# A sum of two lines of g made ahead of pair 2, and an earlier weight set in pair 7, in a four-layer kernel on one core

## The chip, the cores and the metric

The program runs on one core of a Trainium2 chip. The metric is device time in microseconds for one execution. A core has TensorE (PE in the profile), VectorE (DVE), ScalarE (ACT), GpSimd (POOL) and SyncE (SP). Each takes its instructions in the order in which the program gives them, and they wait for one another through semaphores. Transfers are issued by SP and by POOL (a few by ScalarE), each on a queue of its own, and all of them are carried by the same 16 DMA engines. All numbers in this kernel are float32.

## What is computed

x is [1024, 16, 16, 16]. Four layers follow one another, each of them x = x + f(groupnorm(x)) with 8 groups of 2 channels:

```
_gn(v):  g = v.reshape(B, 16, 16, 8, 2); (g - mean) / sqrt(var + 1e-5), over h, w and the 2 channels
layer 0: f = a linear map of the 4096 values of a sample, given as three cores
         core0 [1,16,16,16], core1 [16,16,16,16], core2 [16,16,16,1] (rank, out, in, rank)
layers 1 and 3: per pixel, two 3x3 depthwise filters, 48 -> 128 -> 16 dense with a relu, and a mask
layer 2: a 3x3 convolution over the 16 channels, with a bias
```

The change touches layer 0 and the preparation of layer 3's weights, which happens during layer 0.

## The kernel before

**Layer 0 as products of blocks.** The 4096x4096 matrix of layer 0 is never stored whole. The kernel splits input and output into blocks and needs 26 products of sums of blocks, taken two at a time: 13 *pairs*, numbered from 0, in the table `OUTER`. A pair has four *units* (q = 0 to 3), numbered through, so that unit u = 4 j + q belongs to pair j. A unit makes seven inner products (`INNER`, k = 0 to 6), each in two halves: 14 steps of a unit, numbered 0 to 13, and 56 of a pair (`pieces`, with the matmuls of L1567). One pair takes about 102.5 us.

**The weights of a unit.** What multiplies x is built on the way. From core1 and core2 the kernel makes once, during pair 0, a tensor g that has four *lines* (0 to 3), and stores it in DRAM, in two arrangements: `g_dram[0]` holds lines 0 and 2 side by side, and 1 and 3; `g_dram[1]` holds 0 and 1, and 2 and 3. For a unit, `gload` (L1438, L1440) fetches those lines that the pair's entry in `OUTER` names: a tile of 256 KB holds two lines in its 128 rows. `build` (L1459) multiplies each tile with small coefficients R, made from core0 by `coefs`, and sums over the tiles in PSUM; four copies on ScalarE (L1464) bring the result to SBUF as w. A pair with one or two lines needs one tile in each build, and one with three or four lines needs two: the second goes to a fixed place in the second of the two big tiles of x. There are two builds a unit (h = 0 and 1), for the unit that comes next.

**Sums around the products.** VectorE makes sums of w, s2, s5, s1, s7 and w01 (`mix`, L1489 and L1491), adds the products up from PSUM to r (`gather`, L1603, L1613; some of it is copied by ScalarE, L1609, L1611), and makes a pair's extra inputs from its four blocks of x (`combined`, L1203): E0, E1 and E2, which the fourth to sixth inner products of each unit read, and two blocks changed in place. `combined` of a pair is placed inside its first unit, two operations after each of steps 1, 3, 5, 7 and 9. The result r is stored to the residual xf in DRAM by `store`: from SP the first time (L1543), by an adding transfer from POOL later (L1541). Where a sign or a sum is needed, a `neg` tile is made first (L1527, L1534).

**Work woven in.** `run` gives out the steps of a pair and puts other lists of steps in between, each with a stretch of the pair (`lo` to `hi`, as shares of it); a plain number in such a list is idle time to be kept. So the order of the instructions on each engine is fixed when the program is built. In pair 1 that other work is the second half of the input: 8 loads of 1 MB from POOL's queue (L1074), their statistics on VectorE (BN_STATS, L1086), transposes on TensorE (L1092), copies of them by ScalarE into a `lines` tile (L1102), and stores of these from SP (L1104); and, at its end, `part_steps(2)`, the inputs of pair 2. Tiles with the tag t4 have four buffers of 512 KB in all of layer 0; `lines`, `neg` and `piece` tiles share them. Transposes and builds share PSUM banks: one bank m, and four banks w, all four of which a build takes.

**The weight sets.** `set1` and `set3` are the two lists of steps that prepare the weights of layers 1 and 3 (`nca_weights`); set3 works in the room behind the blocks of x of the even pairs, where E0 to E2 of pair 8 come to stand, and is woven into pair 7 from 0.02 to 0.85 of it. Its last steps are small tensor copies on POOL (`order`, L369), eight stores of zeros to wy (L378), three copies within the room (`copies`, L325), and the stores of pk and kp (`store`, L328 to L330), all on POOL's queue. r of the even units has a fixed place in the same big tile, so that ScalarE's first copy of a unit waits until r of the unit before last has been stored.

## Time and profile before

| | |
|---|---|
| three runs, median | 2743.33 us (2742.66 to 2747.08) |
| the profiled execution | 2746.07 us, of which its span 2744.3 us |
| TensorE, busy | 2675.8 us, 98% of the span |
| VectorE, busy | 1994.9 us, 73% |
| ScalarE, busy | 1241.4 us, 45% |
| pair 1, 185.7 to 288.2 us of the span | TensorE busy for 100.86 of 102.50 us, VectorE for 78.34 |
| pair 2, 288.2 to 391.0 us | TensorE 102.80 of 102.80, VectorE 69.65 |
| DMA | 502.17 MB, 183 GB/s on average |

How to read the profile: a row of a timeline has the start in us from the span's start, how long it took, engine, line, operation, output and inputs, shapes and how many like it stand in a row; in brackets is how long the engine was idle before it, and what released it. Rows of one kind that follow one another closely are merged. Each float32 matmul of the source stands as two matmuls in the trace. A busy share is an average over the whole span, and tells little of any single stage.

### The profile page before, as it was taken

The numbers are of one execution on the slowest core, as the hardware profiler recorded it, in microseconds if no ns is written. First come the engines' busy times: TensorE is split into PE (matmuls) and PEld (weight loads), VectorE is DVE, ScalarE is ACT, GpSimd is POOL, SyncE is SP. The second block draws the span as 40 slices with busy tenths as digits, with TensorE's granted clock in tenths as the row PEclk, the third lists the DMA queues.
The fourth block names the chain that finished last, engine by engine and source line by source line (L and its number), as shares of the span: only waits on it lengthen the run. The fifth ranks groups of instructions, "written<-read, shape, count | busy, mean of one in ns | idle before, by whom it ended". The sixth has DMA issues, their size and how long they took to land.

```text
span 2744.3 us, 47734 instructions
## 1 busy us (share of the span) xinstructions
PE 2675.8 (98%) x19246; PEld 1756.9 (64%) x19246; DVE 1994.9 (73%) x2416; ACT 1241.4 (45%) x2091; POOL 541.3 (20%) x690
## 2 busy tenths in 40 slices
PE   6999999999999999999999999999999999999997
PEld 5888888888888878888778733333333333334344
DVE  8597667867787766667887777658778858756654
ACT  3324222222232222333332276776767756676664
POOL 2000351312122742311331111111113221110000
PEclk8999999999999999999999999999999999999998
DMA  7686788997897687889689764555575866444665
GB/s 254 215 317 227 242 169 214 236 221 188 193 242 193 154 187 180 226 229 263 171 188 257 148 165 102 108 159 122 106 195 83 202 150 143 101 89 116 180 175 209
DMA packets 264796, 502.17 MB, mean 183 GB/s; under 512 B 32804, under 2 KB 100440, under 8 KB 255360
## 3 DMA queue, kind: packets, MB, share of 16 engines
q1 hardware_dynamic: 180752, 338.78, 37.1%
q0 software_dynamic: 83632, 160.22, 33.9%
q8 instruction: 152, 2.49, 0.4%
q14 instruction: 68, 0.56, 0.1%
q10 hardware_dynamic: 192, 0.13, 0.0%
HBM read 280.66 MB, written 223.35 MB: 184 GB/s over the span
## 4 chain that ended last, share of the span: by engine, by line
PE 81%; DVE 8%; DMA 5%; issue 3%; POOL 1%; ACT 1%; SPq 0%; DVEq 0%; POOLq 0%; ACTq 0%
PE po L1567 37%; PE ph L1974 21%; PE po L1803 8%; PE po L1658 5%; PE pw L1459 4%; DMA xn<-in_x_dram 1%; PE po L1667 1%; DVE xn L1174 1%; DMA xf<-r 1%; DMA xn<-xf 1%; DVE xn L1203 1%; PE ptx L1867 1%; DMA L_conv_kp<-xn 1%; DMA xb<-xn 0%; DMA xn<-xn 0%
## 5 line engine op out<-in xcount | busy, mean ns | idle before, releaser
L1977 ACT ACTIVATE hid<-ph,pack 128x512 f32<-128x512 f32 (+1 forms) x1040 | 641.3, 684 | 313.5 <-PE ph L1974 254.3
L1567 PE MATMUL po<-xn,s 128*128 128x256 f32 x3328 | 756.7, 384 | 13.6 <-DVE s L1489 7.2
L1567 PEld LDWEIGHTS po<-xn,s 128*128 128x128 f32 x3328 | 628.5, 191 | 117.5 <-issue 16.7
L1567 PE MATMUL po<-xn,w 128*128 128x256 f32 x2496 | 565.0, 381 | 1.4 <-DVE xn L1203 1.4
L1974 PE MATMUL ph<-xn,wq 32*128 32x512 f32 (+1 forms) x3752 | 518.3, 590 | 1.9 <-DVE u L1815 1.5
L1567 PEld LDWEIGHTS po<-xn,w 128*128 128x128 f32 x2496 | 468.2, 190 | 74.1 <-issue 5.9
L1464 ACT COPY w<-pw 128x512 f32<-128x512 f32 x416 | 213.6, 600 | 454.6 <-PE pw L1459 371.8
L1974 PEld LDWEIGHTS ph<-xn,wq 32*128 32x128 f32 x3752 | 233.6, 184 | 228.9 <-issue 210.0
L1974 PE MATMUL ph<-xn,pack 32*128 32x512 f32 x1288 | 274.2, 607 | 5.6 <-DVE u L1815 1.6
L1489 DVE TENSOR_TENSOR s<-w 128x1024 f32<-128x1024 f32 x208 | 251.2, 1217 | 28.1 <-PE po L1567 24.8
L1803 PE MATMUL po<-hid,pack 128*32 128x512 f32 (+1 forms) x2080 | 256.0, 592 | 0.8 <-ACT hid L1977 0.5
L1815 DVE SCALAR_TENSOR_TENSOR u<-po,pack,xn 128x512 f32<-128x512 f32 (+1 forms) x130 | 96.3, 741 | 168.2 <-PE po L1803 167.1
L1857 POOL DMA_DIRECT2D xf<-u x96 | 82.6, 860 | 618.7 <-DVE u L1855 592.1
L754 DVE TENSOR_TENSOR xn<-xn,m 128x1024 f32<-128x1024 f32 x128 | 150.2, 1217 | 34.7 <-ACT m L777 34.6
L1974 PEld LDWEIGHTS ph<-xn,pack 32*128 32x128 f32 x1288 | 115.6, 184 | 90.7 <-issue 63.1
L1803 PEld LDWEIGHTS po<-hid,pack 128*32 128x32 f32 x2080 | 53.9, 109 | 174.9 <-ACT hid L1977 86.3
L1658 PE MATMUL po<-xn,convw 128*128 128x512 f32 x368 | 163.6, 598 | 0.0
L1203 DVE TENSOR_TENSOR xn<-xn 128x1024 f32<-128x1024 f32 x130 | 152.7, 1215 | 8.0 <-DMA L_conv_kp<-xn 8.0
L1459 PE MATMUL pw<-R,gq 32*128 32x128 f32 x3328 | 143.7, 286 | 7.5 <-DVE small L1116 6.9
L1603 DVE TENSOR_TENSOR r<-r,po 128x1024 f32<-128x1024 f32 x78 | 95.0, 1218 | 72.9 <-PE po L1567 61.0
L1459 PEld LDWEIGHTS pw<-R,gq 32*128 32x128 f32 x3328 | 116.2, 188 | 41.9 <-issue 38.6
L1541 POOL DMA_DIRECT2D xf<-xn x69 | 89.8, 1776 | 251.2 <-DVE xn L1534 71.7
(229 smaller groups left out, 2784.9 us busy)
## 6 DMA issues: line engine op xcount, KB each, us to landing
xn<-xf SPq DMA_DIRECT2D x128, 512.0 KB
xn<-xb SPq DMA_DIRECT2D x36, 1024.0 KB
wq<-L_conv_wy SPq DMA_DIRECT2D x192, 192.0 KB
xf<-xn POOLq DMA_DIRECT2D x69, 512.0 KB, 10.8
piece<-xb SPq DMA_DIRECT2D x64, 512.0 KB
xf<-r POOLq DMA_DIRECT2D x48, 512.0 KB, 12.7
xf<-u POOLq DMA_DIRECT2D x96, 256.0 KB, 4.2
gq<-g_dram SPq DMA_DIRECT2D x94, 256.0 KB
```

The costliest lines, as they stand in the source:

```text
L754: V.tensor_tensor(part, part, m().unsqueeze(1).broadcast_to([P, 2, NB]), op)
L1203: V.tensor_tensor(out, y, z, f)
L1459: T.matmul(pw[r][:, v, i], g[rows, P * (2 * v + i) : P * (2 * v + i) + P], R[rows, k], start=k == 0, stop=k == len(gs) - 1,)
L1464: A.copy(w.rearrange("p b s t m -> p (b s t) m")[:, :, 32 * r : 32 * r + 32].rearrange("p k (v o) -> p v k o", v=2), pw[r].rearrange("p v ...
L1489: V.tensor_tensor(t.rearrange("p s t m -> p (s t m)"), x, y, f)
L1567: T.matmul(po[:, i], matrix(u, what)[:, i, t], x, start=t == 0, stop=t == 3)
L1603: V.tensor_tensor(part, part, po.unsqueeze(2).broadcast_to([P, 2, 2, 256]), ALU.add)
L1658: T.matmul(st["po", h][wh], conv["fw"][:, y], X[:, 16 * wh + h + y - 1], start=y == max(0, 1 - h), stop=y == min(2, S - h),)
L1803: T.matmul(po[32 * j : 32 * j + 32], nca["w1"][:, v], hid[j], start=v == 0, stop=v == 1)
L1815: V.scalar_tensor_tensor(u, po, nca["b1"], X[:, 8 * q + w2, cols(hf)], ALU.add, ALU.add)
L1974: T.matmul(ph, w, x, start=k == 0, stop=k == len(tiles) - 1)
L1977: A.activation(h, ph, AF.Relu, bias=nca["bt"][:, r : r + 1])
```

## The change

Pair 2's entry names lines 0, 1 and 3, and every use of lines 0 and 1 in it has the same coefficient. The changed kernel makes the sum of lines 0 and 1 once and calls it line 4, so that the entry names lines 4 and 3 and a build of pair 2 takes one tile. The sums are made in pair 1, one for each q: two tiles (lines 0 and 2; lines 1 and 3) are fetched from `g_dram[0]` by four transfers of 256 KB on SP into two t4 buffers; one VectorE operation multiplies the first with a constant of each row, `low` (1 in the rows of line 0, and 0 in those of line 2), and adds the second, so that line 0 + line 1 and line 3 stand side by side; two transfers on SP store that to `g_sum`. The four sums are woven into pair 1 from 0.04 to 0.5 of it, with eight us of idle time between each fetch and its sum. `low` is made by one small reduction on VectorE in pair 0. The second part puts the end of set3's stretch in pair 7 from 0.85 to 0.75. Everything else stays as it is, but for the order of woven-in steps that follows from this.

```diff
+    low = cst("low", [P, 1])
...
+    g_sum = dram.tile([4, 2, 4, 2, S, 4 * P], F32, tag="g_sum", name="g_sum")
...
-        ((0, 1, 3), None, ("..++ ..++ .... ....", "+30", "+00 -20"),
+        ((4, 3), None, ("..++ ..++ .... ....", "+30", "+00 -20"),
...
-    UNIT = [(1, 0, 0, 0), (0, 1, 0, 0), (0, 0, 1, 0), (0, 0, 0, 1)]
+    UNIT = [(1, 0, 0, 0), (0, 1, 0, 0), (0, 0, 1, 0), (0, 0, 0, 1), (1, 1, 0, 0)]
...
+        def sum_steps():
+            ts = {}
+            def fetch(q):
+                ts[q] = [
+                    work([P, 2, NB], "t4", name).rearrange("p h b -> p (h b)").rearrange(
+                        "p (o f) -> p o f", o=4
+                    )
+                    for name in ("vs", "vg")
+                ]
+                for h, x in enumerate(ts[q]):
+                    for w in range(2):
+                        nc.sync.dma_start(
+                            x[64 * w : 64 * w + 64],
+                            g_dram[0][h, q, w].rearrange("o s k (t f) -> (s k t) o f", t=2),
+                        )
+            def add(q):
+                t, g = ts[q]
+                V.scalar_tensor_tensor(t, t, low, g, ALU.mult, ALU.add)
+                for w in range(2):
+                    nc.sync.dma_start(
+                        g_sum[q, w].rearrange("o s k (t f) -> (s k t) o f", t=2),
+                        t[64 * w : 64 * w + 64],
+                    )
+            return [
+                x for q in range(4)
+                for x in ((0, lambda q=q: fetch(q)), 8, (1.3, lambda q=q: add(q)))
+            ]
...
-                if pair[1] - pair[0] == 2:
+                if pair == (4, 3):
+                    queue.dma_start(g, g_sum[q, h].rearrange("o s k f -> (o s k) f"))
+                elif pair[1] - pair[0] == 2:
...
+        V.tensor_reduce(low, ident.rearrange("p (w v r) -> p v w r", w=2, v=2)[:, 0], AX.XY, ALU.add)
...
-            (part_steps(2), 0.78, 1.0),
+            (sum_steps(), 0.04, 0.5), (part_steps(2), 0.78, 1.0),
...
-            7: (set3, 0.85),
+            7: (set3, 0.75),
```

In the changed program's own order, the first fetch stands on SP right behind the xf writes of unit 3 (three of 512 KB), and the first sum on VectorE between the w01 mix of unit 4 and the two operations that make E2.

More of the change, by code (lines that the diff above doesn't have):

```diff
@@ L699, in train_setup @@
         ]
-        return sums, cores, early, rest
+        return sums, cores, early, rest, sum_steps
     def line_sum(parts, name, own, dear=False):
@@ L2041, in conv_preact_kernel @@
         stage(es, dict(t4=4, s=2, n=2, w1=1, w0=2, s2=1, s5=1, r=1, gq=2, R=2, A=1), dict(w=4, m=1, o=3))
-        sums, cores, early, rest = train_setup(flats[0][:, 8192:9216])
+        sums, cores, early, rest, sum_steps = train_setup(flats[0][:, 8192:9216])
         tag = ["w"]
```

## The prediction

> **What bounds the kernel now.** I read the page first, then layer 0 alone: the timeline of TensorE (PE), and that of VectorE (DVE) where pair 1 begins. The page says that TensorE is never idle for long:

> ```profile
> PE 2675.8 (98%) x19246; PEld 1756.9 (64%) x19246; DVE 1994.9 (73%) x2416; ACT 1241.4 (45%) x2091; POOL 541.3 (20%) x690
> ...
> PE 81%; DVE 8%; DMA 5%; issue 3%; POOL 1%; ACT 1%; SPq 0%; DVEq 0%; POOLq 0%; ACTq 0%
> ```

> So matmuls taken out of layer 0 count in full, if nothing else comes last there; and whatever makes TensorE wait counts in full too. Timeline of TensorE:

> ```profile
> 64.74 1.17 PE L1459 MATMUL pw<-R,gq 32*128 32x128 f32 x32
> 65.84 1.99 PE L1567 MATMUL po<-xn,s 128*128 128x256 f32 x8
> ...
> 185.75 8.83 PE L1567 MATMUL po<-xn,s 128*128 128x256 f32 x32 [2.80 <-DVE s L1489]
> ...
> 209.47 1.89 PE L1567 MATMUL po<-xn,w 128*128 128x256 f32 x8
> ...
> 214.24 3.62 PE L1567 MATMUL po<-xn,w 128*128 128x256 f32 x16
> ...
> 230.78 1.17 PE L1459 MATMUL pw<-R,gq 32*128 32x128 f32 x32
> ...
> 296.73 0.40 PE L1459 MATMUL pw<-R,xn 32*128 32x128 f32 x8
> 297.06 7.17 PE L1567 MATMUL po<-xn,s 128*128 128x256 f32 x32
> ```

> A build from one tile of g takes 1.10 us from its start to the next matmul (64.74 to 65.84). One of pair 2 starts at 295.06 and ends at 297.06: 2.00 us. Timeline of VectorE early in pair 1, unit 4, which starts at 185.75:

> ```profile
> 202.88 1.22 DVE L1491 TENSOR_TENSOR w<-w 128x1024 f32<-128x1024 f32 x1
> 204.02 2.35 DVE L1203 TENSOR_TENSOR xn<-xn 128x1024 f32<-128x1024 f32 x2
> 206.29 1.22 DVE L1603 TENSOR_TENSOR xn<-xn,po 128x1024 f32<-128x1024 f32 x1
> ```

> It has no idle slot from 165 to 213 us. The pair at 204.02 makes E2, which TensorE wants at 209.47 (step 10). The transfers at that time, queues and their shares, for 196 to 207 us:

> ```profile
> q0 software_dynamic: 493, 3.65, 78.6%
> q1 hardware_dynamic: 492, 0.97, 22.8%
> ```

> All 16 engines are full: POOL's queue carries seven 1 MB loads of x (issued from 181.5 to 187.7, the last landing 21.5 us after its issue), and SP's queue gets 0.97 MB in 11 us.

> [...] 88 KB per us for SP, with 2 KB packets against 8 KB ones, and three xf writes of 512 KB, issued by SP at 192.4, 192.9 and 193.4, have semaphore events that put their landings at 203.6, 209.3 and 210.5. [...] after the 2.80 us of idleness above, 32 matmuls took 8.83 us where 7.17 is usual.

> **The change, part by part.**

> *Builds of pair 2.* Eight builds (4 units by 2 halves) lose one tile of g: 8 x (2.00 - 1.10) = 7.2 us less on TensorE. Pair 2 is bound by it: 102.80 of 102.80 us busy in its window, and VectorE is idle for 33 us of it, so all of this counts. Eight loads of 256 KB go too, and two small VectorE operations of the coefficients; both are hidden, worth 0.

> *The constant `low`.* One TENSOR_REDUCE of 64 values a row: by its nearest row (al_c, 128 values, 0.28 us) about 0.2 us. It stands at 51 us in a stretch where VectorE has no gap and TensorE later waits 1.36 us for it (at 77.38): +0.2.

> *The four sums in pair 1, VectorE's work.* Each is one SCALAR_TENSOR_TENSOR over 128x1024; the nearest row is L1534's, 1.22 us with the next 1.13 behind it. No row has this one's pointer operand and two SBUF inputs; [...] I take 1.14 each, 4.6 in all; from 4 to 6. Alone it would be hidden, as VectorE idles some 24 us in pair 1, all after 213.

> *The first sum's wait.* This is what decides. The sum stands on VectorE right behind the w01 mix (202.88) and ahead of the two E2 operations; its four fetches (1 MB) stand on SP right behind the three xf writes, from about 193.9. In ring order they move after those: the third lands at 210.5, and the fetch at 1.05 MB / 0.39 MB per us (the rate of 209 to 212 us) takes 2.6 more. Call the landing L = 213.1; bounds 211.5 (packets overlapping) and 215. VectorE comes to it at 204.0 and waits 9 us, with E2, a gather, eight BN_STATS and x01 (combined's last) queued behind.
> - E2's first half is done at L + 1.14 + 1.22 = 215.5; TensorE wanted it at 209.47: 6.0 us idle.
> - From E2's start to x01's first half done is 7.2 us (204.02 to 211.26 before): 214.2 + 7.2 = 221.5. TensorE wanted that (step 12) at 214.24: 7.3 us late in all. [...]
> - Mixes and gathers follow in order; s5 of unit 5 is done 17 us after L, when TensorE comes for it: no more.

> *t4 buffers.* Sums and lines share four. By the new program's addresses, the lines tile of the transposes of 226.36 and 228.53 gets the buffer of unit 4's `neg`. That `neg` waits for gathers of the late VectorE: at 231 on ScalarE instead of 220.98. Its fourth xf write was issued 3.3 us later and landed 5.2 after that, so 239.6; then two copies, 240.8. The second copy frees a bank that the next build needs, wanted at 230.78 + 7.4 = 238.2: 2.5 us more. The loss is then 9.9, set by L alone (L - 203.2). Later slots (the other three sums, their stores, the loads of g behind them on SP) come free before they are wanted, by 1 us or more. The last load of x (0.87 us of waiting at 239.65) now shares the engines with 1.5 MB of sums: +0.7. Pair 1: +10.6.

> *set3 sooner.* Ahead of it, pair 8 begins with stalls of 0.79, 2.53, 0.36 and 0.64 us on TensorE (4.3). Their causes, VectorE, ScalarE and POOL:

> ```profile
> 998.30 1.23 DVE L1203 TENSOR_TENSOR xn<-xn 128x1024 f32<-128x1024 f32 x1 [8.01 <-DMA L_conv_kp<-xn]
> ...
> 993.92 0.59 ACT L1609 COPY xn<-po 128x512 f32<-128x512 f32 x1 [16.10 <-DMA xf<-xn]
> ...
> 969.17 2.48 POOL L1541 DMA_DIRECT2D xf<-xn  x2 [2.10 <-ACT w L1464]
> 972.45 1.19 POOL L1541 DMA_DIRECT2D xf<-xn  x1 [0.81 <-DMA L_conv_wy<-xn]
> 980.11 0.61 POOL L328 DMA_DIRECT2D L_conv_pk<-xn  x1 [6.46 <-DMA xn<-xn]
> ```

> The step that stores pk and kp now stands ahead of those three xf writes on POOL, behind one xf<-xr more. It must still wait for copies whose queue of small wy writes is the limit (60 to 70 GB/s at a full DMA share, 960 to 970 us). POOL reaches wy 6.6 us sooner, but the xf<-r writes in front end 3 us later, so the copies land some 2 to 3 us sooner; xf<-xr (0.5 MB) takes that up. Then 1.0 MB of stores and 1.5 MB of xf writes are left, as before, in the other order: kp is early, and VectorE's 8.01 us goes; but the last xf write lands where kp did, near 1000.5 instead of 993.8, and ScalarE's copy (16.10) waits for it. TensorE's step 6 of unit 32, ready at 994.3, starts at 1001.7: 7.4 us of idleness in the place of 4.3, +2.9 or so, and a halved window, +1.7. Bounds: -4.3 (all four stalls go) and +8; I take +4.6.

> *Sum:* -7.2 + 0.2 + 10.6 + 4.6 = +8.2 us. The profiled execution took 2746.07 (span 2744.3, 1.8 around it), 2.7 above the median of the three runs, so +8.2 means 2754.3 for one like it and 2751.5, say 2751, for the median.

> **Rivals.**
> - *The saving stands.* The fetch is in time, so sums hide in VectorE's gaps: needs L below about 205.5. Then -7.2, with 0 to -4.3 from pair 7: 2732 to 2737. For it: sums are only 4.6 us of work. Against: three earlier writes of the same ring land at 203.6 to 210.5. It ends faster. Chance 0.12.
> - *Pair 7 pays.* Pair 1 loses as forecast, but POOL's stores and the xf writes both land before 994: 10.8 - 7.2 - (0 to 4.3) = -1 to +4: 2743 to 2747. It needs the copies to land at about 970. For it: POOL is free sooner; against: wy's rate. Chance 0.20.
> - *A milder first wait*, L near 209 [...]: +6 - 7.2 + 4.6, about +3, 2747. Chance 0.08.
> - *More stalls*: a second buffer or bank cascade, further half-clock windows: above +15, 2759 and more. Chance 0.06.

> **How the numbers follow.** The forecast (2749 to 2757) has 0.54. Something under 5.5 us (0.2%) can't be told from no change by this measurement. Faster 0.12; same 0.20 + 0.08 = 0.28; slower 0.54 + 0.06 = 0.60. The range leaves out the first rival and the last one: 2740 to 2759.

> **What would show it.** A wait of 8 to 10 us on VectorE before its first sum, near 204 us; TensorE idle some 6 us before step 10 of unit 4, then at step 12; PEclk below 1 there; a wait of ScalarE for xf writes near 235 and of a build near 238; builds of pair 2 at 1.10 us; at pair 8's start no wait for kp, and a longer one of ScalarE for xf<-xn. I am wrong if the first sum starts by 206, or if TensorE has no stall where pair 8 begins.

## The result, and the profile after

The changed kernel takes 2750.1 us in the median (2748.34 to 2754.25), the kernel before 2743.44 beside it (2739.81 to 2754.0), in 22 runs each: 1.0022 times as long, with an interval of 1.0016 to 1.0029. It is slower by 4 to 8 us, where +8 was forecast. The profiled execution has a span of 2748.7 us, 4.4 more than that of before; the rest of the difference is in the executions that happened to be profiled, since that of before was 2.6 above its median. Executions of one kernel differ by several us (by 14 in the 22 of before), and a trace is one of them: it shows where that execution lost time, and the ratio of many executions what the kernel takes.

TensorE has less work and more idle time. From the page, the busy times and the chain that ended last:

```profile
PE 2670.0 (97%) x18990; PEld 1751.1 (64%) x18990; DVE 1999.5 (73%) x2419; ACT 1241.7 (45%) x2091; POOL 528.0 (19%) x690
...
PE 82%; DVE 8%; DMA 5%; issue 3%; SPq 1%; ACT 1%; POOL 0%; DVEq 0%; ACTq 0%; POOLq 0%
```

Timeline of TensorE after (start, us, engine, line, operation; in brackets the idle time before, and what ended it). In the changed file the lines named here are 34 to 36 higher: L1603 was L1567, L1495 was L1459, L1126 was L1092.

```profile
208.94 0.65 PE L1126 MATMUL ptin<-ident,xn 128*128 128x128 f32 x4
216.66 3.52 PE L1603 MATMUL po<-xn,w 128*128 128x256 f32 x8 [7.06 <-DVE xn L1237]
...
239.59 0.50 PE L1495 MATMUL pw<-R,gq 32*128 32x128 f32 x6
243.35 1.81 PE L1495 MATMUL pw<-R,gq 32*128 32x128 f32 x26 [3.27 <-ACT lines L1136]
...
308.47 1.17 PE L1495 MATMUL pw<-R,gq 32*128 32x128 f32 x32
309.58 2.64 PE L1603 MATMUL po<-xn,s 128*128 128x256 f32 x11
...
898.97 0.50 PE L288 MATMUL L_conv_pt<-ident,xn 128*16 128x128 f32 x3 [1.67 <-DMA xn<-in_L_conv_fc_w_dram]
...
992.22 7.07 PE L1603 MATMUL po<-xn,s 128*128 128x256 f32 x32
999.13 3.62 PE L1603 MATMUL po<-xn,w 128*128 128x256 f32 x16
1002.67 1.17 PE L1495 MATMUL pw<-R,gq 32*128 32x128 f32 x32
1003.78 7.17 PE L1603 MATMUL po<-xn,s 128*128 128x256 f32 x32
```

Five things stand there. Step 10 of unit 4 waits for 7.06 us. A build stops in its middle for 3.27 us. A build of pair 2 takes 1.11 us (308.47 to 309.58). A new wait of 1.67 us stands at set3's first transpose in pair 7. And pair 8 (992.22) begins without any of the four stalls that it had before. The longest of those four, in the timeline of TensorE before:

```profile
999.58 1.99 PE L1567 MATMUL po<-xn,s 128*128 128x256 f32 x8 [2.53 <-DVE xn L1203]
```

What the wait before step 10 comes from is in the timeline of VectorE after, and what stops the build is in that of ScalarE after:

```profile
202.40 1.22 DVE L1527 TENSOR_TENSOR w<-w 128x1024 f32<-128x1024 f32 x1
214.18 1.28 DVE L718 SCALAR_TENSOR_TENSOR vs<-vs,low,vg 128x1024 f32<-128x1024 f32 x1 [10.56 <-DMA vg<-g_dram]
215.38 2.35 DVE L1237 TENSOR_TENSOR xn<-xn 128x1024 f32<-128x1024 f32 x2
```

```profile
232.19 1.06 ACT L1563 ACTIVATE neg<-xn 128x1024 f32<-128x1024 f32 x1 [1.90 <-DVE xn L1639]
...
242.22 1.07 ACT L1136 COPY lines<-ptin 128x512 f32<-128x512 f32 x2 [5.78 <-DMA xf<-neg]
```

VectorE stands for 10.56 us in front of the first sum, with E2 behind it. The late VectorE delays `neg` (232.19, before at 220.98), its xf write lands at 242.07, and only then may ScalarE write `lines` in the same t4 buffer and free a bank for the build. Around or behind each of the two waits TensorE runs at half its clock. The windows view of the changed kernel has, for each stretch, the busy times of PE, PEld, DVE, ACT and POOL with their instructions, then PEclk (the share of the clock that was granted), DMA share and GB/s:

```profile
212.90:219.80 6.90, 3.15 (x8) 2.53 (x9) 5.62 (x8) 0.00 (x0) 0.00 (x0) 0.51 0.61 167
...
243.60:247.10 3.50, 3.50 (x35) 3.28 (x32) 0.93 (x1) 2.06 (x4) 0.38 (x1) 0.51 1.07 340
```

To see where the time went I compare one kind of mark in the two traces, the first of ScalarE's copies (w from pw) of a unit's first build. Unit 4's mark lies 0.31 us earlier than before, unit 8's 12.52 later, unit 13's 7.49, unit 29's 7.80, unit 31's 9.58 and unit 34's 4.44. So pair 1 lost 12.8 us up to this mark, which lies 0.9 behind the first shorter build; up to unit 13 it got 5.0 back, which is about what seven more shorter builds (0.9 each, 6.3) leave behind a new wait of 0.99 at 352.95; pair 7 lost 1.8, most of it set3's transpose; and the start of pair 8 gave 5.1 back. Counted by its 56 steps, pair 1 runs from 185.75 to 313.17 in the trace before and pair 2 to 428.68: both are longer than the 102.5 us given above, and the two windows of the table there end inside them. Two of pair 2's eight shorter builds lie in pair 1 (before, at 295.06 and 304.17).

### The profile page after: what moved, and what is told of

Read it like the earlier page. It is cut to its first block, busy times and chain, and to the rows that moved or that the text cites. A ratio compares the mean times of both kernels' runs of the same rounds, so it can differ in the third digit from the quotient of the medians.

```text
span 2748.7 us, 47252 instructions
## 1 busy us (share of the span) xinstructions
PE 2670.0 (97%) x18990; PEld 1751.1 (64%) x18990; DVE 1999.5 (73%) x2419; ACT 1241.7 (45%) x2091; POOL 528.0 (19%) x690
## 4 chain that ended last, share of the span: by engine, by line
PE 82%; DVE 8%; DMA 5%; issue 3%; SPq 1%; ACT 1%; POOL 0%; DVEq 0%; ACTq 0%; POOLq 0%
PE po L1603 39%; PE ph L2010 21%; PE po L1839 8%; PE po L1694 5%; PE pw L1495 4%; DMA xn<-xf 1%; DMA xn<-in_x_dram 1%; PE po L1703 1%; DMA xn<-xr 1%; DMA m<-means 1%; DVE xn L1208 1%; PE ptx L1903 1%; DVE s L1525 1%; DMA xb<-xn 0%; DVE u L1851 0%
## 5 line engine op out<-in xcount | busy, mean ns | idle before, releaser
L1603 PE MATMUL po<-xn,s 128*128 128x256 f32 x3328 | 754.6, 383 | 11.4 <-DVE s L1525 8.7
L1603 PEld LDWEIGHTS po<-xn,s 128*128 128x128 f32 x3328 | 627.8, 191 | 113.8 <-issue 16.0
L1603 PE MATMUL po<-xn,w 128*128 128x256 f32 x2496 | 566.9, 382 | 8.7 <-DVE xn L1237 8.7
L1603 PEld LDWEIGHTS po<-xn,w 128*128 128x128 f32 x2496 | 469.2, 190 | 82.4 <-DVE xn L1237 9.2
L1495 PE MATMUL pw<-R,gq 32*128 32x128 f32 x3328 | 140.8, 287 | 11.0 <-DVE small L1150 7.1
L1495 PEld LDWEIGHTS pw<-R,gq 32*128 32x128 f32 x3328 | 115.0, 189 | 45.5 <-issue 38.5
```

Of the source, the lines that this page charges most:

```text
L1495: T.matmul(pw[r][:, v, i], g[rows, P * (2 * v + i) : P * (2 * v + i) + P], R[rows, k], start=k == 0, stop=k == len(gs) - 1,)
L1603: T.matmul(po[:, i], matrix(u, what)[:, i, t], x, start=t == 0, stop=t == 3)
```

## Experiments

In the expectations theories have letters.

- For set3: A, putting it sooner is what takes pair 8's stalls away; B, the step of the forecast, by which it costs 4.6 us; C, the stalls went because TensorE comes there later.
- For pair 1: A, the forecast's, VectorE's wait for a fetch that is late by its place in SP's ring (SP's queue, whose transfers stand in the order of their issue); D, the fetch is late because of the loads of x on POOL's queue, wherever it stands; F, the sums' t4 buffers.
- Waits that an edit could bring: E, for xf writes that come later; G, of TensorE for other inputs, beside the sums' transfers; H, for loads of x that are moved back.

Each kernel was timed beside the kernel before on the same chip, in four groups on four chips, with 5 to 14 runs; so compare the ratios, and medians only roughly. The table gives the ratio to the kernel before with its interval, and from the one profiled execution the lateness in us that arises between two marks: in pair 1 (units 4 to 8), in pair 2 (8 to 13), in pair 7 (29 to 31) and where pair 8 begins (31 to 34).

| | median | ratio | interval | pair 1 | pair 2 | pair 7 | pair 8 |
|---|---|---|---|---|---|---|---|
| the change | 2750.1 | 1.0022 | 1.0016 to 1.0029 | +12.8 | -5.0 | +1.8 | -5.1 |
| sums, set3 at 0.85 | 2749.86 | 1.0016 | 1.0006 to 1.0026 | +14.1 | -6.0 | 0.0 | -2.3 |
| set3 at 0.75 alone | 2743.94 | 1.0000 | 0.9992 to 1.0008 | +1.0 | 0.0 | +1.4 | -5.1 |
| fetch ahead of xf writes | 2750.45 | 1.0022 | 1.0011 to 1.0033 | +10.8 | -5.2 | +1.5 | -5.1 |
| first sum later | 2747.64 | 1.0013 | 1.0005 to 1.0021 | +8.9 | -5.5 | +1.6 | -5.1 |
| loads of x behind fetch | 2746.28 | 1.0007 | 0.9999 to 1.0015 | +7.8 | -4.8 | +1.3 | -5.1 |
| a place of its own | 2754.88 | 1.0035 | 1.0023 to 1.0047 | +16.5 | -5.5 | +1.4 | -5.1 |
| sums from 0.26 | 2742.29 | 0.9995 | 0.9987 to 1.0003 | +5.9 | -5.7 | +1.5 | -5.1 |
| from 0.26, own place | 2742.35 | 0.9993 | 0.9985 to 1.0001 | +4.7 | -6.1 | +2.0 | -5.1 |
| spread into pair 2 | 2755.31 | 1.0037 | 1.0023 to 1.0051 | +5.4 | +6.9 | +1.7 | -5.1 |
| the same, set3 at 0.85 | 2753.22 | 1.0037 | 1.0023 to 1.0052 | +4.7 | +6.8 | 0.0 | -5.1 |
| behind the last load | 2746.66 | 1.0006 | 0.9997 to 1.0014 | +7.7 | -5.7 | +1.6 | -5.1 |
| the same, set3 at 0.85 | 2744.93 | 1.0004 | 0.9996 to 1.0013 | +7.4 | -6.2 | 0.0 | -5.1 |

The kernel with set3 alone has no edit in pair 1 and shows +1.0 there (it waits 0.90 us for a load of x at 202.09), so differences of 1 us in that column mean nothing. Nor is a trace the total: the span of the last kernel's profiled execution is 4.7 us shorter than that of before, and its ratio is 1.0004.

### Each part alone

The sums without the earlier set3:

```diff
-            7: (set3, 0.75),
+            7: (set3, 0.85),
```

> The sums as in the changed kernel, set3 back at 0.85. In the trace of the changed kernel, pair 1 costs 13.9 us, the builds of pair 2 give 7.2 back, and pair 8 begins without the 4.3 us of stalls that it had before, at the price of one new stall of 1.67 us at set3's first transpose. Theory A (putting set3 sooner is what took pair 8's stalls away): the stall at 899 us goes, 4 us of stalls stand at pair 8's start again, and the time is 1 to 4 us above the changed kernel: 2751 to 2754. Theory B, the forecast's step (set3 sooner costs 4.6): 4.6 us below the changed kernel, about 2745.5. Theory C (pair 8's stalls went because TensorE comes there some 8 us later, while POOL's chain does not shift): no stalls at pair 8's start here either, and about 1.7 below the changed kernel, 2748.

And the earlier set3 without the sums, in the kernel before:

```diff
-            7: (set3, 0.85),
+            7: (set3, 0.75),
```

> The kernel before with set3 at 0.75 alone, no sums. Theory A (set3 sooner takes pair 8's stalls away): pair 8 begins with at most 1 us of stalls in the place of 4.3, TensorE waits up to 1.7 us at set3's first transpose near 890 us, and the time is 2 to 4 us below the kernel before: 2739.5 to 2741.5. Theory B, the forecast's step: a wait of ScalarE for an xf write in the place of VectorE's for kp, 7.4 us idle at step 6 of unit 32, 4.6 us slower: 2748. Theory C (TensorE's lateness in the changed kernel did it): within 1.5 us of the kernel before.

The sums alone have most or all of the change's loss (1.0016 times, +4.4 us, from 1.6 to 7.1). Their time lies between those that C (2748) and A (2751 to 2754) named, and so does their trace, with 2.0 us of stalls where pair 8 begins; B's 2745.5 is 4.4 below it. Set3 alone measures 1.0000 with an interval of 2.2 us to each side: the forecast's +4.6 (B) is refuted, and so is a gain of more than 2.2. Its trace has what A said, no stall where pair 8 begins and 1.33 us at the first transpose (893.65), but its time is what C named, and not the 2 to 4 us less of A. Of POOL's chain the traces show two things. pk and kp, now in front of the xf writes, land early, and the xf writes too: in the changed kernel pk and kp at 976.7 to 978.2 and the last xf write at 986.7, against 996.3 to 1000.5 and 993.8 before. And six small selects on POOL, which began 8 us later than before, ended 1 us sooner. Timeline of POOL, before and then after:

```profile
896.39 12.66 POOL L279 TENSOR_SCALAR_AFFINE_SELECT xn<-xn 48x256 f32<-48x256 f32 x6
```

```profile
904.20 3.87 POOL L280 TENSOR_SCALAR_AFFINE_SELECT xn<-xn 48x256 f32<-48x256 f32 x6
```

The single records are 3.78, 0.39, 0.39, 4.78, 1.85 and 1.34 us before, and 0.90, then four of 0.39, and 1.26 after. The one of 4.78 runs from 901.06 to 905.84; what VectorE did then is in its timeline before:

```profile
899.84 1.20 DVE L1603 TENSOR_TENSOR xn<-xn,po 128x1024 f32<-128x1024 f32 x1
900.97 1.21 DVE L1242 TENSOR_TENSOR xn<-xn 128x1024 f32<-128x1024 f32 x1
902.11 1.21 DVE L1518 TENSOR_TENSOR xn<-xn 128x1024 f32<-128x1024 f32 x1
903.25 1.21 DVE L1242 TENSOR_TENSOR xn<-xn 128x1024 f32<-128x1024 f32 x1
904.38 1.21 DVE L1489 TENSOR_TENSOR s<-w 128x1024 f32<-128x1024 f32 x1
905.65 0.61 DVE L299 TENSOR_SCALAR xn<-L_conv_pf,xn 48x384 f32<-48x384 f32 x1
```

Two selects of 0.39 us went by while VectorE added from PSUM (899.84). The next one took 4.78 and ended only when four additions in a row with both inputs in SBUF were over (900.97 to 905.59). It isn't always so: the select at 901.06 did not, in a chain of four, but in the changed kernel the last one (906.80 to 908.07) ended in the middle of two additions that took 2.56 us together, where 2.34 is usual (897.57 before). Timeline of VectorE after:

```profile
906.59 2.56 DVE L1525 TENSOR_TENSOR s<-w 128x1024 f32<-128x1024 f32 x2
```

No run isolates it, as no kernel moved the selects alone.

But the earlier place isn't what the stalls of pair 8 hang on. Four kernels have set3 at 0.85, all with selects of 12 to 13 us: their stalls at pair 8's start are 4.3 (before), 2.0, 0 and 0 us. Nor is it TensorE's lateness alone (C): their pair 8 begins at 982.64, 992.16, 994.31 and 983.76. At 0.85 the stores and the xf writes land near the time at which they are wanted: kp at 1000.5 in the kernel before, and at 994.5 in the last of the four, though its copies had landed only 0.6 to 1.7 us sooner. What makes these 6 us was not isolated. At 0.75 none of ten traces has a stall. What the early place costs in return is in all ten, a wait of 1.2 to 1.9 us at set3's first transpose in pair 7. In the totals the two places can't be told apart (the last two pairs of rows of the table).

### Why the fetch is late

The forecast had the fetch wait for its turn behind three xf writes. So the fetch goes ahead of them; in the list of woven-in steps the first fetch gets the position 0.0 and all others keep theirs:

```diff
-            (sum_steps(), 0.04, 0.5), (part_steps(2), 0.78, 1.0),
+            *[([f], at, 1.0) for two, ats in zip(sum_steps(), zip((0.0, 0.155, 0.27, 0.3851), (0.1148, 0.2298, 0.3448, 0.4598))) for f, at in zip(two, ats)], (part_steps(2), 0.78, 1.0),
```

with `sum_steps` returning the pairs of fetch and sum. The kernels below that give positions one by one do it in the same way.

> The changed kernel with one edit: the four transfers of the first fetch stand on SP ahead of the three xf writes of unit 3, not behind them; the first sum keeps its place on VectorE. Theory A, the forecast's (what makes the first sum wait is that its fetch is behind 1.5 MB of writes in SP's ring, while the loads of x take most of the engines): the fetch is issued near 186 and has landed by 203, the first sum waits at most 1 us, TensorE has no stall before step 10 of unit 4 nor the one before the build near 243, and of pair 1's 13.9 us 3 or less stay: 2739 to 2741.5. Rival D (the fetch is slow by itself beside the loads of x, wherever it stands): it takes 18 us again, lands at 204 to 206, the sum waits 1 to 3 us, and about 2743. Rival E (the xf writes, now some 10 us later, make somebody wait): the first wait goes, and a wait for an xf write comes, 2745 or more.

Both A and the numbers of D missed. Issued at 184.96 to 187.47, ahead of the xf writes, the four transfers land at 203.15, 209.18, 211.64 and 212.30, and VectorE still waits:

```profile
212.43 1.28 DVE L718 SCALAR_TENSOR_TENSOR vs<-vs,low,vg 128x1024 f32<-128x1024 f32 x1 [8.39 <-DMA vg<-g_dram]
```

So an issue that is 8.5 to 11.5 us earlier bought 1.7 us. TensorE's 7.06 us before step 10 are gone, but it waits 2.20 us for a load of x (201.47) and 2.72 in the middle of the build before that step (214.86), whose `lines` copy stands behind the sum. The transfers of 196 to 207 us say why, for the changed kernel and then for this one (queue, packets, MB, share of 16 engines):

```profile
q0 software_dynamic: 492, 3.59, 77.5%
q1 hardware_dynamic: 519, 1.02, 23.8%
```

```profile
q0 software_dynamic: 484, 3.53, 87.7%
q1 hardware_dynamic: 482, 0.47, 14.4%
```

In each of these two kernels the two queues move nearly the same number of packets, whatever is in them, as they did in the kernel before (493 and 492). The prediction has those two numbers, and didn't draw the consequence: against POOL's packets (7.3 KB in the mean), xf writes in packets of 2 KB get 93 KB per us (1.02 MB in the 11 us), and the fetch, in packets of 1 KB, 43 (0.47 MB). Moved to the front, the fetch has its turn in the time in which the ring carries least. What ends that time is the last load of x (209.05 in the changed kernel, 211.87 in this one): in the changed kernel SP's queue moved 1.02 MB in the 11 us up to 207 and 0.95 MB in the 3 us from there, with 0.09 MB left on POOL's. The next run takes the loads away instead. Three of the seven are issued by SP behind the fetch:

```diff
-            queue.dma_start(
+            (nc.sync if (n, half) == (1, 1) and bg < 3 else queue).dma_start(
...
-            steps_of(phases[1]), 107, (), ([(0, x) for x in loads[:7]] + [8] + woven_in + tail, 0.0, 0.76),
+            steps_of(phases[1]), 107, (), ([(0, x) for x in loads[:4]] + [8] + woven_in + tail, 0.0, 0.76), ([(0, x) for x in loads[4:7]], 0.06, 1.0),
```

> The changed kernel with one edit: three of the seven loads of x that POOL's queue carries at the start of pair 1 (3 MB) are issued by SP in their place, behind the first fetch; everything else keeps its order. After the run with the fetch ahead of the xf writes the theory is D: SP's ring gets little of the 16 engines until the loads of x on POOL's queue have landed (209 us), so what stands in the ring's way matters less than these loads. Theory D: with 4 MB on POOL's queue these end near 197, xf writes and fetch follow at full rate, the fetch has landed by 204, the first sum waits at most 1 us, neither the 7 us of TensorE before step 10 of unit 4 nor the 3.27 before the build is there, and 2737 to 2740. Rival A, the forecast's (ring order behind 1.5 MB of writes at SP's own rate, about 90 KB per us): the fetch still lands after 209, TensorE waits 5 us or more, 2746 to 2750. Rival H (the x loads behind come late for the transposes): the first wait goes, and 2 to 4 us of TensorE waiting for x come, 2741 to 2744.

Transfers of 196 to 207 us, and the timelines of VectorE and TensorE:

```profile
q1 hardware_dynamic: 1961, 3.09, 93.3%
q0 software_dynamic: 93, 0.63, 13.6%
```

```profile
207.98 1.29 DVE L718 SCALAR_TENSOR_TENSOR vs<-vs,low,vg 128x1024 f32<-128x1024 f32 x1 [3.68 <-DMA vg<-g_dram]
```

```profile
210.45 2.00 PE L1603 MATMUL po<-xn,w 128*128 128x256 f32 x8 [0.61 <-DVE xn L1237]
...
218.49 1.97 PE L1126 MATMUL ptin<-ident,xn 128*128 128x128 f32 x8 [3.88 <-ACT lines L1136]
```

With 4 MB on POOL's queue the fetch lands at 207.85, 6.2 us sooner, with the three xf writes still in front of it. TensorE's 7.06 us are 0.61. D holds in this: the loads of x on the other queue made most of the first wait. Its numbers missed (the fetch by 204, VectorE waiting 1 us at most, 2737 to 2740), and no run has both these loads and the xf writes out of the fetch's way. Pair 1 loses 7.8 all the same, since `lines` now waits for the sum's store (TensorE's 3.88 us at 218.49), and TensorE for the last load of x (1.76 us, H).

### t4 buffers

Here the first sum stands on VectorE behind x01 and two gathers, with the fetch unmoved (its position 0.2 in the place of 0.1148):

> The changed kernel with one edit: the first sum stands on VectorE behind x01 and two gathers of unit 4 in the place of ahead of E2; its fetch stays where it is on SP. Theory A (all that pair 1 loses, the 7 us before step 10, the half clock, the later stall of 3.27 before a build, comes from VectorE's wait for the first fetch): the sum waits less than 0.5 us, none of these stalls is there, pair 1 costs 0 to 2 in the place of 13.9: 2736 to 2738.5. Rival F (the later stall belongs to the sums' t4 buffers and transfers, not to the first wait): 3 us idle before the build near 236 stay, 2739 to 2741. Rival G (transfers of the sums cost TensorE's other inputs as much): above 2743.

The wait before step 10 is gone, as A said, and pair 1 still loses 8.9, so that the time is where G had it, above 2743. The greater part is F: the tiles are held longer instead, and ScalarE's `lines` wait, once for the sum and once for the store of earlier `lines`, in this kernel's timeline of ScalarE:

```profile
218.38 1.07 ACT L1136 COPY lines<-ptin 128x512 f32<-128x512 f32 x2 [4.37 <-DVE vs L718]
225.99 1.08 ACT L1136 COPY lines<-ptin 128x512 f32<-128x512 f32 x2 [6.53 <-DMA xr<-lines]
```

They pass it on to transposes (2.64 and 1.67 us of TensorE at 219.02 and 226.62). The rest is G: TensorE waits 0.99 and 1.98 us for loads of x (202.24 and 250.82). Then one of the two tiles of each sum was put elsewhere:

```diff
-                    work([P, 2, NB], "t4", name).rearrange("p h b -> p (h b)").rearrange(
+                    (work([P, 2, NB], "t4", name).rearrange("p h b -> p (h b)") if name == "vg" else flats[1][:, 15360:16384]).rearrange(
```

> The changed kernel with one edit: the first of the two tiles of each sum stands in the free kilobyte floats of the second big tile of x in the place of a t4 buffer, so that a sum holds one t4 buffer and not two. Theory F (the later stalls of pair 1 come through the t4 buffers): the first wait, 7 us of TensorE, stays; the 3.27 us before the build near 243 go or fall under 1; 2746 to 2748.5. Rival: they come from the late VectorE alone, the 3.27 stay, within 1 us of the changed kernel, 2749 to 2751. It may also be that one fetch now waits for the store of the sum before, which has the same place: then VectorE waits 3 us or more for its second or third sum.

The stall of 3.27 us in the build is gone. But r of unit 3 lies in that place until its xf writes have landed, so that the fetch is issued at 212.27, and VectorE waits 14.52 us for it, and TensorE 10.29 before step 10. The run says nothing clean on the share of the buffers.

### Is there a place for the sums

From 0.26 to 0.72 of pair 1, when the first loads of x have landed (`(sum_steps(), 0.26, 0.72)`), then the same with the tile in a place of its own, free by then:

> The changed kernel with the four sums spread from 0.26 to 0.72 of pair 1 in the place of 0.04 to 0.5, so that the first fetch is issued when the loads of x have landed. Theory D: each fetch takes 5 to 7 us, the first sum doesn't wait, no stall before step 10 of unit 4; pair 1 costs at most 3 of the 13.9 us; 2737.5 to 2741. Rival F (two t4 buffers held from fetch to store are what costs, wherever the sums stand): transposes or builds wait 4 to 8 us in all for ScalarE's lines copies, 2742 to 2746.

> Both edits: the sums from 0.26 on, and the first tile of each in a place of its own, so that a sum holds one t4 buffer. If theories D and F both hold, pair 1 costs at most 1 to 2 us, and what is left is the 7.2 of the builds of pair 2 and set3's 1 to 4: 2735 to 2738, ahead of both kernels by 5 us or more. If the sums' other costs (1.3 us of VectorE each, 1.5 MB of transfers each) count on the path, 2739 to 2742.

No wait before step 10, and no stall by `lines` of more than 0.51 us: by their ratios both are 7 to 8 us below the changed kernel. Against the kernel before they are 0.9995 and 0.9993, which this measurement can't tell from no change, and pair 1 loses more than the 3 and the 2 us expected. They differ from each other by 1.2 us there, so the second t4 buffer makes no clear difference at this place. In both, pair 1 loses most in one wait, here from TensorE's timeline of the first:

```profile
243.89 1.33 PE L1126 MATMUL ptin<-ident,xn 128*128 128x128 f32 x5 [4.03 <-DMA xn<-in_x_dram]
```

The last load of x took 9.53 us from its issue, against 6.36 before, beside the transfers of the sums. I took it for the second fetch, and moved the second and third sum to 0.56 and 0.70 of pair 1, and the fourth to 0.03 of pair 2 (with set3 at 0.75 and at 0.85):

> The changed kernel with the sums spread by the traffic: the first fetched at 0.26 of pair 1 (the loads of x have landed), the second at 0.56 and the third at 0.70 (behind the last load of x, which TensorE waited 4.0 us for when the second fetch stood beside it), the fourth at 0.03 of pair 2. Theory D (what the sums cost is the collision of their transfers with the loads of x): the last load lands some 6 us after its issue, TensorE waits at most 1 us for it, pair 1 costs at most 2 us, and with the 7.2 of the builds and 1 to 3 from set3 the time is 2735 to 2738, 6 us or more below the kernel before. Rival F (two t4 buffers a sum, somewhere): a wait for lines or for a piece of pair 2's inputs comes back, 2739 to 2742.

> The same spread with set3 back at 0.85. If set3 at 0.75 spares pair 8's stalls (4.3 us of idleness and what a half clock adds, less 1.4 at set3's first transpose), this is 1.5 to 4 us above the spread with 0.75, its GpSimd selects take 8 us or more in the place of 4 to 5, and pair 8 begins with 2 to 4.3 us of stalls. If set3's place is worth nothing where TensorE runs as early as in the kernel before, the two agree within 1 us.

The first expectation failed; of the second's two cases the ratios, 1.0037 both times, fit the one in which set3's place is worth nothing. The load still landed 9.28 us after its issue: what pushes it back is the first sum, whose fetch lets four xf writes land at 232.4 to 236.2 (in the kernel before, 1.6 us ahead here, at 225.4 to 229.5) and whose store lands at 240.7 and 241.3, beside the load. And the fourth sum holds up pair 2, which loses 6.9 us where the changed kernel got 5.0 back. Timelines of VectorE and TensorE:

```profile
339.60 1.29 DVE L718 SCALAR_TENSOR_TENSOR vs<-vs,low,vg 128x1024 f32<-128x1024 f32 x1 [4.75 <-DMA vg<-g_dram]
...
354.57 1.23 DVE L1208 TENSOR_TENSOR xn<-xn 128x1024 f32<-128x1024 f32 x1 [6.28 <-DMA xn<-xr]
```

```profile
343.21 8.86 PE L1603 MATMUL po<-xn,w 128*128 128x256 f32 x32 [3.65 <-DVE xn L1237]
...
357.67 2.90 PE L1603 MATMUL po<-xn,s 128*128 128x256 f32 x6 [5.60 <-DVE s L1525]
```

It is the first sum of pair 1 over again: the fetch behind four xf writes, a wait of VectorE, then block loads of 1 MB that stand on SP behind the sum's store. The last placement has all sums behind the last load of x and ahead of those block loads, fetched at 0.46, 0.54, 0.62 and 0.70, each sum 0.075 later:

> The changed kernel with all four sums behind the last load of x, and ahead of pair 3's block loads: fetches at 0.46, 0.54, 0.62 and 0.70 of pair 1, each sum 0.075 later. In the two runs before this one the last load of x was still 3.8 to 4.0 us late, because the first sum's fetch and store stood beside it, and the fourth sum in pair 2 made VectorE wait 4 to 5 us and then for block loads behind its transfers. Theory D (a sum costs what its 1.5 MB of transfers push back): now no load of x is pushed back, TensorE waits for the last one no more than 1 us, as in the kernel before, pair 1 costs at most 2 us, and with 7.2 from the builds and about 3 from set3: 2735 to 2738. Rival F (t4 buffers): a wait of ScalarE for lines or of pair 2's pieces, 2739 to 2743. If the block loads of pair 2 are pushed back by the fourth sum, VectorE waits in pair 2: above 2743.

> The same with set3 back at 0.85. If set3's earlier place is worth what the trace of set3 alone shows at pair 8's start (3.7 us), this run is 2 to 4 us above the one with 0.75, with pair 8's stalls of 4.3 us back and GpSimd's six selects at 10 us or more in all. If its place is worth nothing in the total, the two agree within 1 us, about 4 us or more below the kernel before by the builds alone.

The last load is in time (TensorE waits 0.72 us for it), which fits that the first sum's transfers had pushed it back, and F takes the place. The first time is above what D and F had (2735 to 2743), and neither is 4 us below the kernel before. Timelines of ScalarE and TensorE in the first of the two:

```profile
267.59 1.07 ACT L1136 COPY lines<-ptin 128x512 f32<-128x512 f32 x2 [5.20 <-DMA xf<-neg]
```

```profile
268.23 1.97 PE L1126 MATMUL ptin<-ident,xn 128*128 128x128 f32 x8 [4.38 <-ACT lines L1136]
```

So pair 1 lost 4.7 to 16.5 us in every placement, to waits that changed with the placement. None of the runs beats the kernel before by more than the measurement can tell.

## Why the prediction was right, and where it wasn't

*Builds of pair 2, -7.2:* right; 1.11 us each (forecast 1.10), and the change shows from mark to mark.

*`low`, +0.2:* not shown. The wait of 1.36 us at 77 became 1.64, but in the kernel with set3 alone, which has no `low`, it is 2.33.

*Four sums on VectorE:* one takes 1.28 us, not the 1.14 that I estimated; a TENSOR_TENSOR of this size took 1.22 (202.40). The sums were hidden, but for the first.

*The first sum's wait:* the mechanism was right, in its order: fetch, VectorE, E2, step 10. L was 214.0 (forecast 213.1), since the four transfers behind the xf writes went at 1.05 MB in 3.8 us (0.27 MB per us) where the forecast took 0.39. VectorE waited 10.56 (9), TensorE 7.06 (6.0). The second wait, at step 12, didn't come: step 10 ran at half clock, 3.52 us in the place of 1.89, and took it up; step 12 came 9.3 late (7.3). The reason given for L, the place in the ring behind three xf writes, was only half of it: without these in front the fetch landed at 212.3, and without three of the loads of x on the other queue at 207.9. That L came within 1 us is in part luck.

*t4 buffers:* the chain of `neg`, xf write, `lines` and build was right link by link: 232.2 (231), 242.1 (239.6), 3.27 us of idleness (2.5). What the step left out is the half clock behind it, 3.4 us of it, 1.7 lost. The wait of 2.63 us at 185.27 was followed by half clock too. The last load of x, for which 0.7 was added, gave 0.7 back. With that, pair 1 cost 13.9 from its first matmul to the first shorter build (308.47 against 295.06, after a start 0.48 sooner), where 10.6 was the sum: the term for L was too small, and the sum has none for half clock.

*set3 sooner, +4.6:* wrong, in sign for the profiled execution (-5.1 and +1.8) and refuted for the total (1.0000, at most +2.2). The step that failed is "POOL reaches wy 6.6 us sooner, but ... the copies land some 2 to 3 us sooner; the last xf write lands where kp did". wy was issued 8.5 us sooner in absolute time and the copies landed 10.7 sooner, while TensorE came 9.6 later; the last xf write landed at 986.7, not 1000.5. Its rival, "pair 7 pays", had this mechanism, with the condition that it named (copies at about 970: they landed at 968.8).

*The total:* +8.2 forecast, +6.7 in the medians, +4.4 in the two profiled spans. Errors of +3.3 in pair 1, of -7.9 for set3 in the profiled pair, and of 1.0 in a new wait at 352.95 make the 4.4 (8.2 + 3.3 - 7.9 + 1.0 = 4.6). They partly made up for one another: that the median came within 1 us of the forecast is luck as far as set3 goes. Apart, and in many executions, the sums alone took 4.4 us (1.6 to 7.1) where the forecast had 3.6, and set3 alone 0.0 (2.2 to each side) where it had 4.6.

## What to carry to other kernels

Price a transfer that feeds an in-order engine by when it lands. Beside POOL's loads of x the rate of SP's queue went with the size of its packets (93 KB per us with packets of 2 KB, 43 with 1 KB): work out a transfer's share against what the other queue carries then, before asking where it stands in its own ring. Work "in idle time" still needs buffers and transfers: here 1.5 MB of transfers and one or two of four buffers for each sum cost 4.7 us or more of the 7.2 saved, in each placement that was run. Where a few chains meet within some us, as at pair 8's start, one trace shows a stall, another none, and only many executions tell what an edit there is worth.
